# Two attention layers on one core: the result's stores move from GpSimd's queue to SyncE's, and one weight tile moves in SBUF

## The chip, the cores and the metric

The kernel runs on one core of a Trainium2 chip. The metric is the device time of one execution in microseconds; of each kernel several executions are timed and their median is given. A core has five engines that run their own instruction streams: TensorE (PE, matrix products), VectorE (DVE), ScalarE (ACT), GpSimd (POOL) and SyncE (SP). They meet through semaphores. DMAs are issued by an engine's instruction and carried out by 16 DMA engines that all queues share; in this kernel SP and POOL issue all of them.

## The reference

Input is `x`, 48 x 48 positions of 768 channels, in float32. Two layers follow each other, each of the form `x = x + attention(group_norm(x))`, the norm over 32 groups of 24 channels. The attention has 12 heads of 64 channels over all 2304 positions, with two tables of relative positions:

```python
qkv = x @ qkv_w + qkv_b
u = x @ FacTu_w                                   # layer 0 only, rank 16
qkv[..., :C] += u @ q_facts_w @ FacTv_w
qkv[..., 2*C:] += u @ v_facts_w @ FacTv_w
attn = einsum('bqc,bkc->bqk', q * scale, k)
attn += rel_h[:, :, :, :, None] + rel_w[:, :, :, None, :]   # from q and the tables
out = softmax(attn) @ v
return out @ proj_w + proj_b
```

Layer 0 adds low-rank terms to the q and v weights (a 768 x 16 matrix, a 16 x 16 one, a 16 x 768 one). Layer 1 has none; there the weights come transposed.

## The kernel before

`two_layers` (line 56) calls `compute` (line 72) once for the fast form "f". That form takes exponentials without subtracting the maximum first; it stores the reciprocals of the denominators and at the end judges from them whether they all lie in a safe range: `judge` (line 1081) writes one number, `bad`. Every engine loads `bad` (line 63) and branches on it (line 67). Only when it isn't zero does a second form "g" run, with the maxima subtracted. In the runs here it is skipped: each engine jumps over its instructions. Behind the jump, the other side of the branch sets the semaphores to what the skipped form would have left them at: each engine waits for its own semaphore (SP for those of its DMAs, POOL for those of its own) and raises them. Then the program ends: SP waits for all of them (line 1337), and all engines meet in two barriers.

A layer has these stages. In layer 0, `load_transposed` brings `x` in and turns it so that channels lie on the 128 partitions. `group_norm` normalises; `project` computes k and v; `project_q` (line 601) computes q and, from q and the tables, the position terms for rows (`psr`, stored by `rel_h`) and for columns (`psc`, stored by `rel_w`, lines 663 to 684, at the very end of each half of the heads). All of k, v, q and the position terms go to DRAM through POOL's queue. `attend_plain` (line 861) then runs over 6 pairs of heads and, for each pair, 5 blocks of up to 512 queries. A block needs key rows in two float parts (`k`), the queries in two parts (`q`) and three `rel` tiles of position terms, one for each group of 768 keys (`NG` = 3, index g). `fetched` (line 951) issues these loads on SP in the order g = 0, 1, 2; for the first block the keys come in the same three steps. `Block.scores` (line 971) uses `rel[b // 2]`, so that the third `rel` tile serves the last 6 of the 18 key tiles of a block. `out_project` (line 1120) multiplies with `proj_w`, adds the residual, and in layer 1 turns the result back and stores it.

The two sets of buffers of the attention, `in0` and `in1`, reuse memory that earlier stages have left. Pools with `reuse_waits` wait tile by tile: a load into a tile waits for the last readers and writers of the tiles that lay at the same bytes before, and of no others. So where a tile lies decides whom a later load waits for. SP executes its instructions in order, and each of its DMAs signals on one of 8 semaphores in turn; a DMA waits until the one eight places before it has landed.

`Weights` (line 255) holds the small tiles of a layer in a pool of one buffer for each tag, `p0_one`; memory is given out in the order in which tags are first asked for. `begin` (line 276) asks for fu, facts and fv of the low-rank terms, then bt (biases) and for both tables flat and tab, which the position products read until the end of `project_q`. `low_rank` (line 312) multiplies the low-rank factors into `low`, 128 x 2 x 768 numbers, 6144 bytes of each partition; `fold` (line 363) uses `low` to add the low-rank terms to the v and q weights; its last use is in the middle of the first half of `project_q`. `begin` is called again for layer 1, after layer 0's attention.

In the built program the tiles of layer 0 in `p0_one`, and the first attention block's `rel` tiles, lie at these bytes of each partition:

| tile | before |
|---|---|
| fv | 217728 to 220800 |
| bt, flat0, tab0 | 220800 to 222040 |
| flat1, tab1 | 222048 to 223192 |
| low | 223200 to 229344 |
| rel, second group | 214976 to 221120 |
| rel, third group | 221120 to 227264 |
| bt, flat, tab of layer 1 | 226944 to 229336 |

In the last layer `out_project` takes the blocks of 384 positions in three rounds of two. In a round, PE forms seven products for each of three channel tiles; then for each of the 2 x 3 groups of 128 positions PE turns the six channel tiles into `psn`, ACT copies them to a tile `o` of 128 x 768 (six buffers), and POOL issues the store to `out`:

```python
o = op.tile([P, C], F32, tag="o", name=f"o_{b}_{i}_{j}")
nc.scalar.copy(o, ps[:, 0:C])
nc.gpsimd.dma_start(out[ts(pair[i] * TPB + j, P), :], o)
```

All loads of the three rounds stand on SP ahead of this in the built program; the stores are POOL's last DMAs.

Of the kernel before, what the change touches and what calls it, by code (L numbers as in the profile page):

```python
# [9 lines left out]
F32 = mybir.dt.float32  # L10
# [8 lines left out]
P = 128  # L19
C = 768  # L20
# [8 lines left out]
TPB = QB // P  # L29
# [42 lines left out]
def compute(ctx: ExitStack, tc: tile.TileContext, x, layers, out, run, bad):  # L72


    nc = tc.nc
# [22 lines left out]
    for sign, base in ((1, 0), (-1, GSZ - 1)):  # L98
        nc.gpsimd.affine_select(
            out=gin, in_=gin, compare_op=ALU.is_ge, fill=0.0, base=base,  # L100
# [3 lines left out]
            out=gout, in_=gout, compare_op=ALU.is_ge, fill=0.0, base=base,  # L104
# [25 lines left out]
    with ExitStack() as hots:  # L130
# [4 lines left out]
        for i, (rows, pattern, shape) in enumerate(parts):  # L135
# [3 lines left out]
                out=t, in_=t, compare_op=ALU.not_equal, fill=1.0, base=0,  # L139
# [18 lines left out]
    def in_order(instruction):  # L158

        tc.keep_in_program_order(instruction)  # L160
# [94 lines left out]
    class Weights:  # L255
# [20 lines left out]
        def begin(self):  # L276
            one, ly = self.one, self.ly
            if ly.lora is not None:
                u_w, q_f, v_f, o_w = ly.lora
                self.fu = one.tile([P, CT, RANK], F32, tag="fu", name="fu")  # L280
                nc.gpsimd.dma_start(self.fu, u_w.rearrange("(t p) r -> p t r", p=P))
                self.facts = one.tile([RANK, 2, P], F32, tag="facts", name="facts")
                nc.gpsimd.memset(self.facts, 0.0)
                self.out = one.tile([P, C], F32, tag="fv", name="fv")
                for i, f in enumerate((q_f, v_f)):
                    nc.gpsimd.dma_start(self.facts[:, i, 0:RANK], f)
                for r in range(4):
                    nc.gpsimd.dma_start(self.out[r * 32 : r * 32 + RANK, :], o_w)
            self.bt = one.tile([P, 3 * CT], F32, tag="bt", name="bt")
            nc.sync.dma_start(self.bt, ly.qkv_bt)  # L290
            nc.sync.dma_start(v_bias[self.li], ly.qkv_bt[:, 2 * CT :])

            self.tables = []
            for a, src in enumerate((ly.relh_t, ly.relw_t)):
                flat = one.tile([P, REL], F32, tag=f"flat{a}", name=f"flat{a}")
                tab = one.tile([P, REL, 2], F32, tag=f"tab{a}", name=f"tab{a}")
                nc.gpsimd.memset(tab, 0.0)
                for par in range(2):  # L300
                    nc.sync.dma_start(flat[ts(par, HD), :], src)
                self.tables.append((flat, tab))
# [9 lines left out]
        def low_rank(self, room):  # L312


            if self.ly.lora is None:
                return
            fuT = room.tile([RANK, C], F32, tag="x", name="fuT")
            self.low = self.one.tile([P, 2, C], F32, tag="low", name="low")
            for r in range(1, 4):
                nc.gpsimd.tensor_copy(  # L320
                    self.facts[:, :, r * 32 : r * 32 + RANK], self.facts[:, :, 0:RANK]
                )
            for half in range(2):
                cols = ts(half, HP * P)
                ps = self.ps.tile([P, HP * P], F32, tag="f", name=f"psu_{half}")
                for t in range(HP):
                    in_order(nc.tensor.transpose(
                        ps[0:RANK, ts(t, P)], self.fu[:, half * HP + t, :], ident
                    ))
                nc.vector.tensor_copy(fuT[:, cols], ps[0:RANK])  # L330
            for half in range(2):
                yield
                cols = ts(half, HP * P)
                for i in range(2):
                    ps = self.ps.tile([P, HP * P], F32, tag="f", name=f"psl_{half}_{i}")
                    in_order(nc.tensor.matmul(
                        ps, lhsT=self.facts[:, i, :], rhs=fuT[:, cols], start=True, stop=True
                    ))
                    nc.scalar.copy(self.low[:, i, cols], ps)
# [521 lines left out]
    def attend_plain(li, qd, kd, vd, rel_d, od, beside):  # L861
# [11 lines left out]
        with ExitStack() as es:  # L873
# [166 lines left out]
                            self.rec[r * HD : r * HD + 1, :],  # L1040
                        )


            wanted = [fetch_keys(0), fetch_values(0), fetch_queries(0, *blocks[0])]
            keys, queries, v = fetched(wanted[0], wanted[2], wanted[1])
            behind = []
# [73 lines left out]
    def out_project(ly, li, od, w, bt, first, res, xT, next_res, beside):  # L1120


        last = xT is None
        with ExitStack() as es:
            tp = es.enter_context(tc.tile_pool(name="p3_t", bufs=1, **REUSE))
            kp = es.enter_context(tc.tile_pool(name="p3_k", bufs=2, **REUSE))
            rp = es.enter_context(tc.tile_pool(name="p3_r", bufs=2, **REUSE))
            yp = es.enter_context(tc.tile_pool(name="p3_y", bufs=2, **REUSE))
            ps_y = es.enter_context(tc.tile_pool(
                name="ps_y", bufs=4 if last else 8, space=PSUM, **REUSE  # L1130
            ))
            ps_n = None
            if last:
                op = es.enter_context(tc.tile_pool(name="p3_o", bufs=2 * TPB, **REUSE))
                ps_n = es.enter_context(tc.tile_pool(name="ps_n", bufs=2, space=PSUM, **REUSE))
            for at, b in enumerate((1, 0, 2)):
                pair = (b, b + HB)
                if last and not shifted and at == HB - 1:
                    judge(ps_n)
                if not last:  # L1140
                    y = [xT[i] for i in pair]
                elif at == 0:
                    y = first[2:]
                else:
                    y = yp.tile([P, 2, CT, QB], F32, tag="y", name=f"y_{b}")
                    y = [y[:, i] for i in range(2)]
                if at == 0:
                    oT = first[:2]
                else:
                    oT = rp.tile([P, 2, CT, QB], F32, tag="oT", name=f"oT_{b}")  # L1150
                    oT = [oT[:, i] for i in range(2)]
                for i in range(2):
                    fetch_output(oT[i], od, pair[i])

                for i in range(2):
                    nc.sync.dma_start(y[i], res[pair[i]])
                if at == 0:
                    next(beside, None)
                blocks = {
                    f"{i + 1}{j + 1}": oT[j][:, i * HP : (i + 1) * HP]  # L1160
                    for i in range(2) for j in range(2)
                }
                t = tp.tile([P, 4, HP, QB], F32, tag="t", name=f"oT_t_{b}")
                right = sums_of_b(blocks, t)
                for co in range(HP):
                    def product(i):
                        left_of, right_of = FACTORS[i]
                        ps = ps_y.tile([P, QB], F32, tag="y", name=f"psy_{b}_{co}_{i}")
                        for t in range(HP):
                            nc.tensor.matmul(  # L1170
                                ps, lhsT=w[left_of][:, t, ts(co, P)], rhs=right[right_of][:, t, :],
                                start=(t == 0), stop=(t == HP - 1),
                            )
                        return ps

                    def result(at, x, more):
                        i, j = int(at[0]) - 1, int(at[1]) - 1
                        ch = i * HP + co
                        to = y[j][:, ch, :]
                        nc.vector.tensor_add(to, to, more)  # L1180
                        nc.vector.scalar_tensor_tensor(
                            to, x, bt[:, ch : ch + 1], to, ALU.add, ALU.add
                        )
                        if not last:
                            nc.vector.bn_stats(stats[:, ch, pair[j], :], to)

                    seven_products(kp, QB, product, result)
                for _ in beside:
                    pass
                for i in range(2):  # L1190
                    if not last:
                        nc.gpsimd.dma_start(next_res[pair[i]], y[i])
                        continue
                    for j in range(TPB):
                        ps = ps_n.tile([P, 1024], F32, tag="n", name=f"psn_{b}_{i}_{j}")
                        for t in range(CT):
                            nc.tensor.transpose(ps[:, ts(t, P)], y[i][:, t, ts(j, P)], ident)
                        o = op.tile([P, C], F32, tag="o", name=f"o_{b}_{i}_{j}")
                        nc.scalar.copy(o, ps[:, 0:C])
                        nc.gpsimd.dma_start(out[ts(pair[i] * TPB + j, P), :], o)  # L1200

    residuals = [[scratch(f"res{li}_{b}", [P, CT, QB]) for b in range(NQB)] for li in range(2)]
    def begin(li, es):
# [137 lines left out]
```

## Time and profile before

| | us |
|---|---|
| median of 3 runs | 3338.63 (3338.19 to 3340.41) |
| the profiled execution, its own time | 3338.02 |
| its span, first to last instruction | 3336.3 |
| PE busy | 3258.2 (98%) |
| POOL busy | 382.8 (11%) |
| first store of the result issued on POOL, last | 3223.2, 3316.7 |
| last instruction of SP that loads data | 3196.3, for 1.7 |
| PE's wait for `rel` in the first block of layer 0 | 4.8 |

The profile shows one execution. Its own time is 1.7 us over the span of its instructions. Busy time of PE is taken from the records of its products; issuing a DMA isn't counted as busy on SP, and a semaphore wait isn't counted on any engine. In lists of groups, "A <- B" names what an instruction writes and reads, "SPq" or "POOLq" an instruction of that engine's sequencer. A DMA has two times: how long its issue held the engine, and when it landed. "L1200" is line 1200 of the kernel before.

### The profile page before, as it was taken

To read this page: it belongs to the slowest core of one execution; us is meant where nothing else is said; L and a number is where in the kernel's file an instruction comes from. 1 tells how busy PE (TensorE), PEld (TensorE's weight loads), DVE (VectorE), ACT (ScalarE), POOL (GpSimd) and SP (SyncE) were. 2 spreads that over 40 slices of the span, in tenths; PEclk is the share of its full clock that TensorE was granted. 3 is DMA by queue.
4 is the path that set the end of the run, shared out by engine and by line. 5 is a ranking of instruction groups with operands and counts; after the bars stand their busy time and mean duration, and the time that the engine had idled before them with its cause. 6 is when DMAs were issued, how large, how long until landed. Compare 5 with 4: busy or idle time off the path is not lost.

```text
span 3336.3 us, 50056 instructions
## 1 busy us (share of the span) xinstructions
PE 3258.2 (98%) x19708; PEld 2002.1 (60%) x19708; DVE 2103.0 (63%) x2275; ACT 1422.4 (43%) x1655; POOL 382.8 (11%) x719
## 2 busy tenths in 40 slices
PE   8999999999999999999989999999999999999997
PEld 5556665565656565656555566656565656565654
DVE  8432446777777677777774234677777767767653
ACT  3101345555555555553011024655555555555511
POOL 2144110000000000000012531100000000000000
PEclk9999999999999999999999999999999999999998
DMA  7333479453436353425234346863534444533241
GB/s 261 128 85 84 135 226 250 85 111 93 121 74 141 73 125 90 106 64 172 86 135 137 56 120 201 244 158 89 123 82 125 90 119 94 121 83 86 86 145 58
DMA packets 221202, 405.60 MB, mean 122 GB/s; under 512 B 41584, under 2 KB 109072, under 8 KB 217120
## 3 DMA queue, kind: packets, MB, share of 16 engines
q1 hardware_dynamic: 178656, 253.00, 31.1%
q0 software_dynamic: 42304, 149.31, 14.0%
q8 instruction: 159, 2.61, 0.3%
q14 instruction: 83, 0.68, 0.1%
HBM read 253.27 MB, written 148.89 MB: 121 GB/s over the span
## 4 chain that ended last, share of the span: by engine, by line
PE 85%; issue 7%; ACT 2%; DVE 2%; DMA 2%; POOL 1%; SPq 1%; POOLq 0%; ACTq 0%; DVEq 0%
PE ps_sc L960 33%; PE ps_ov L960 25%; PE ps_q L695 8%; PE ps_v L521 7%; PE ps_k L521 4%; PE psy L1170 4%; ACT pt L987 1%; PE psr L635 1%; PE ps_d L960 1%; DMA rel<-f_r 1%; PE psc L635 1%; POOL f_k L565 1%; DVE relw L390 0%; ACT relw L389 0%; POOL out_dram L1200 0%
## 5 line engine op out<-in xcount | busy, mean ns | idle before, releaser
L993 DVE TENSOR_TENSOR sum<-sum,pt 128x1024 f32<-128x1024 f32 (+1 forms) x960 | 1072.6, 1117 | 317.2 <-ACT pt L987 233.6
L987 ACT ACTIVATE pt<-ps_sc 128x1024 f32<-128x1024 f32 (+1 forms) x1080 | 990.6, 939 | 660.6 <-PE ps_sc L960 600.4
L960 PE MATMUL ps_sc<-q,k 64*128 64x512 f32 (+1 forms) x8640 | 1096.3, 373 | 9.6 <-ACT pt L987 8.1
L960 PEld LDWEIGHTS ps_sc<-q,k 64*128 64x128 f32 x8640 | 774.2, 185 | 273.8 <-issue 92.0
L960 PE MATMUL ps_ov<-pt,v 128*64 128x512 f32 (+1 forms) x4320 | 883.9, 554 | 0.0
L960 PEld LDWEIGHTS ps_ov<-pt,v 128*64 128x64 f32 x4320 | 293.5, 137 | 475.2 <-issue 436.1
L960 PE MATMUL ps_sc<-rel,places 64*128 64x512 f32 (+1 forms) x2160 | 412.3, 371 | 4.8 <-DMA rel<-f_r 4.8
L695 PE MATMUL ps_q<-xT,w_q 128*128 128x384 f32 x864 | 285.5, 489 | 0.6 <-DVE v L585 0.6
L1038 POOL DMA_DIRECT2D f_rec<-rec x120 | 58.3, 490 | 1951.2 <-DVE rec L1027 1950.9
L1027 DVE RECIPROCAL rec<-ps_d 128x512 f32<-128x512 f32 (+1 forms) x60 | 182.2, 3036 | 100.0 <-PE ps_d L960 100.0
L960 PEld LDWEIGHTS ps_sc<-rel,places 64*128 64x128 f32 x2160 | 211.2, 185 | 34.4 <-DMA rel<-f_r 5.1
L695 PEld LDWEIGHTS ps_q<-xT,w_q 128*128 128x128 f32 x864 | 163.2, 191 | 110.4 <-issue 2.9
L599 POOL DMA_DIRECT2D f_v<-v x288 | 137.3, 485 | 105.8 <-DVE v L585 94.2
L701 DVE TENSOR_SCALAR x_q<-ps_q,bt 128x384 f32<-128x384 f32 x72 | 44.4, 617 | 163.3 <-PE ps_q L695 163.3
L521 PE MATMUL ps_k<-xt,w_k 128*128 128x384 f32 x432 | 143.4, 487 | 3.6 <-DVE xt L425 2.6
L521 PE MATMUL ps_k<-xT,w_k 128*128 128x384 f32 x324 | 116.2, 512 | 4.7 <-DVE xT L248 4.6
L521 PEld LDWEIGHTS ps_k<-xt,w_k 128*128 128x128 f32 x432 | 81.5, 190 | 63.0 <-PE ps_k L521 3.0
L1002 ACT CAST sum<-sum 128x1024 bf16<-128x1024 f32 (+1 forms) x60 | 57.6, 960 | 132.3 <-DVE sum L993 132.3
L1005 DVE TENSOR_TENSOR sum<-sum,sum 128x1024 bf16<-128x1024 f32 (+1 forms) x60 | 67.1, 1119 | 61.6 <-ACT sum L1004 61.6
L1003 DVE TENSOR_TENSOR sum<-sum,sum 128x1024 f32<-128x1024 f32 (+1 forms) x60 | 67.1, 1119 | 61.6 <-ACT sum L1002 61.6
L993 DVE TENSOR_TENSOR sum<-pt 128x1024 f32<-128x1024 f32 (+1 forms) x60 | 67.1, 1118 | 47.3 <-ACT pt L987 46.2
L384 ACT ACTIVATE xs_q<-x_q 128x1152 fp32r<-128x1152 f32 x24 | 27.9, 1164 | 161.5 <-DVE x_q L701 153.6
(186 smaller groups left out, 2416.9 us busy)
## 6 DMA issues: line engine op xcount, KB each, us to landing
rel<-f_r SPq DMA_DIRECT2D x1152, 96.0 KB, 4.1
f_k<-xs POOLq DMA_DIRECT2D x72, 384.0 KB, 2.9
f_q<-xs_q POOLq DMA_DIRECT2D x48, 576.0 KB, 3.8
k<-f_k SPq DMA_DIRECT2D x72, 384.0 KB, 5.8
q<-f_q SPq DMA_DIRECT2D x96, 256.0 KB, 3.0
f_r<-relh POOLq DMA_DIRECT2D x48, 432.0 KB, 5.0
f_r<-relw POOLq DMA_DIRECT2D x8, 2592.0 KB, 18.2
f_v<-v POOLq DMA_DIRECT2D x288, 48.0 KB, 2.0
```

The costliest lines, as they stand in the source:

```text
L521: nc.tensor.matmul(ps, lhsT=x, rhs=y, start=(t == 0), stop=(t == HP - 1))
L599: nc.gpsimd.dma_start(vd[to : to + KG, :], v[ts(r, KG), k])
L635: nc.tensor.matmul(ps[:, i, :, :], lhsT=weights.tables[a][:, 2 * s : 2 * (s + HG)], rhs=lines_of(l0 + i), start=True, stop=True,)
L695: nc.tensor.matmul(ps, lhsT=w[:, t, ts(pr, P)], rhs=xT[b][:, t, :], start=(t == 0), stop=(t == CT - 1),)
L960: in_order(nc.tensor.matmul(*args, **kwargs))
L987: nc.scalar.activation(pt, ps[:, :, 0 : self.n], AF.Exp)
L993: nc.vector.tensor_add(self.sum, self.first if kt == 1 else self.sum, pt)
L1003: nc.vector.tensor_sub(self.sum, self.sum, hi)
L1005: nc.vector.tensor_sub(lo, self.sum, mid)
L1027: nc.vector.reciprocal(self.rec, ps)
L1038: nc.gpsimd.dma_start(recs[li][2 * self.pair + r : 2 * self.pair + r + 1, to], self.rec[r * HD : r * HD + 1, :],)
L1170: nc.tensor.matmul(ps, lhsT=w[left_of][:, t, ts(co, P)], rhs=right[right_of][:, t, :], start=(t == 0), stop=(t == HP - 1),)
```

## The change

Two things are changed. The 18 stores of the result are issued by SP in place of POOL. And the tile `low` is asked for in `Weights.begin`, ahead of bt and the tables, in place of `low_rank`, so that it lies at bytes 220800 to 226944 and bt, flat and tab of layer 0 lie behind it, at 226944 to 229336, where those of layer 1 lie too. What is computed, and the order of the instructions on PE, DVE and ACT, stays; so does the size of the pool. In the new file, lines 285 to 317 stand one lower down, and those behind line 1042 one higher up.

```diff
@@ -282,6 +282,7 @@
                 self.facts = one.tile([RANK, 2, P], F32, tag="facts", name="facts")
                 nc.gpsimd.memset(self.facts, 0.0)
                 self.out = one.tile([P, C], F32, tag="fv", name="fv")
+                self.low = one.tile([P, 2, C], F32, tag="low", name="low")
                 for i, f in enumerate((q_f, v_f)):
                     nc.gpsimd.dma_start(self.facts[:, i, 0:RANK], f)
                 for r in range(4):
@@ -315,7 +316,6 @@
             if self.ly.lora is None:
                 return
             fuT = room.tile([RANK, C], F32, tag="x", name="fuT")
-            self.low = self.one.tile([P, 2, C], F32, tag="low", name="low")
             for r in range(1, 4):
                 nc.gpsimd.tensor_copy(
                     self.facts[:, :, r * 32 : r * 32 + RANK], self.facts[:, :, 0:RANK]
@@ -1197,7 +1196,7 @@
                             nc.tensor.transpose(ps[:, ts(t, P)], y[i][:, t, ts(j, P)], ident)
                         o = op.tile([P, C], F32, tag="o", name=f"o_{b}_{i}_{j}")
                         nc.scalar.copy(o, ps[:, 0:C])
-                        nc.gpsimd.dma_start(out[ts(pair[i] * TPB + j, P), :], o)
+                        nc.sync.dma_start(out[ts(pair[i] * TPB + j, P), :], o)
```

## The prediction

> **What bounds the kernel now.** I read the page first, then the chain of waits by stretches, then the two places that the change touches: the end of the program and the start of layer 0's attention. Line 1 of the page says that PE bounds nearly everything; a change to DMAs counts only where PE waits for one, or after PE's last product.
>
> ```profile
> span 3336.3 us, 50056 instructions
> PE 3258.2 (98%) x19708; PEld 2002.1 (60%) x19708; DVE 2103.0 (63%) x2275; ACT 1422.4 (43%) x1655; POOL 382.8 (11%) x719
> ```
>
> PE is idle for 3336.3 - 3258.2 = 78 us. The timeline's last rows put 20 us of that at the end: after ACT's copy at 3315.56 + 0.80 = 3316.36 nothing but stores and sequencer work is left. The stores' own view, and the views of lines 67 and 1337 (the end of the branch on `bad`, the end of the program; a "q" marks a sequencer's instruction, the numbers are ns min/median/max, then first and last start):
>
> ```profile
> L1200 POOL DMA_DIRECT2D out_dram<-o x18: 539/539/549, 3223.2 to 3316.7; - x18
> DMA to landing us min/median/max: 2.6/3.8/5.6
> ...
> L67 SPq EVENT_SEMAPHORE  x8: 17/17/17, 3277.5 to 3278.0; - x8
> L67 POOLq EVENT_SEMAPHORE  x5: 17/43/43, 3321.8 to 3322.4; - x5
> L67 SPq COMPARE_BRANCH  x1: 45/45/45, 3273.3 to 3273.3; - x1
> L67 POOLq COMPARE_BRANCH  x1: 54/54/54, 3317.8 to 3317.8; - x1
> L67 POOLq INC_SWDGE_SEM  x1: 2682/2682/2682, 3322.5 to 3322.5; - x1
> ...
> L1337 SPq EVENT_SEMAPHORE  x14: 17/28/28, 3325.1 to 3336.2; - x14
> L1337 POOLq DRAIN  x3: 46/107/10277, 3325.2 to 3336.0; - x3
> ```
>
> The reader is to see the tail as a row: the last store is issued at 3316.65 and lands 5.6 us later, at 3322.25; only then do POOL's five waits end (3322.4); then come INC_SWDGE_SEM, 2.68 us, and a DRAIN of 10.28 us (3325.16 to 3335.44); the last barriers take 3336.3 - 3335.5 = 0.8 us. Some 13 us stand on POOL alone, after everything has landed. SP passed its own eight waits of line 67 already at 3278.
>
> At the other place (SP's timeline, its waits from 495 to 530 us, PE's timeline):
>
> ```profile
> 501.04 1.73 SPq L897 DMA_DIRECT2D k<-f_k  x2
> 504.33 0.32 SPq L941 DMA_DIRECT2D rel<-f_r  x1
> 506.59 1.11 SPq L945 DMA_DIRECT2D rel<-f_r  x1
> 508.57 1.61 SPq L941 DMA_DIRECT2D rel<-f_r  x1
> 510.22 2.06 SPq L945 DMA_DIRECT2D rel<-f_r  x1
> ...
> SPq L941 <- PE psc L635: 1.5, 1, 1.5
> ...
> 529.94 0.76 PE L960 MATMUL ps_sc<-rel,places 64*128 64x512 f32 x1 [4.83 <-DMA rel<-f_r]
> ```
>
> SP waits 1.5 us for the last position product before it loads the third group of the first block's rel rows; PE later waits 4.83 us for the last of these eight loads.
>
> **What the Trainium skill says.** "DMA: Bandwidth & Descriptors", section "Latency and other measured facts", gives a first byte after about 0.6 us for SP's path and 1 us for POOL's. In this trace's DMA packets the first data starts 0.95 us after an undisturbed issue on SP (q at 470.24) and 1.12 us after POOL's at 3312.42: same order, a smaller gap. Its section "Queues, rings and completion order" has each DMA engine take turns between queues by packets; the trace agrees: while POOL's 27648-byte packets of `f_r<-relw` move (about 1.1 us each), SP's queue falls from 155 packets per us (at 507 us) to between 6 and 20 (510 to 521). "Runtime: NRT & Kernel Launch", "Instruction fetch mechanics": a taken branch out of the fetched pages waits for a fetch. Here the next instruction stands 4.0 us after POOL's branch and 4.1 after SP's. "VectorE: DVE Perf Modes", "The DRAIN you can't avoid", knows boilerplate DRAINs of about 12 ns on all engines; that holds for SP, ACT, DVE and PE here (7 to 17 ns), not for POOL's 10277 ns, and the trace decides.
>
> **The change part by part.** The order of work on PE, DVE and ACT is untouched; 18 stores leave POOL's program and stand behind SP's last load.
>
> *Stores, the way there.* SP issues its last load at 3196.3 and the first store is due at 3223, so no load stands behind a store. Each needs one issue on SP (0.3 to 0.45 us, rows of the k and rel loads) against ACT's two copies per 1.77 us: it keeps pace. ACT's copies wait for buffers of an earlier round, which landed some 40 us before. The first two rounds lie beside PE's products: 0.
>
> *Stores, the last round.* POOL's first issue came 0.29 us after its copy (3312.13 to 3312.42); SP's releases take 0.02 us, and the first data comes 0.17 us sooner: data starts about 0.45 us earlier. The six stores are 2.36 MB. The three rounds took 8.66, 8.75 and 9.83 us from first issue to last landing on POOL; six key loads of the same shape on SP took 8.9 (2692.49) to 9.7 us (2345.94). I take 9.3: 3312.15 + 9.3 = 3321.4, against 3322.25. No store on SP is in this trace; bounds 8.5 and 14 us (POOL's 3072-byte packets of `f_v<-v` took 268 ns in the mean; six stores are 48 such packets per DMA engine, 12.9 us).
>
> *SP's own way out* is now behind the last store: issue 3316.4 to 3316.85, load of `bad` 0.79 (its time before), branch 0.05, fetch 4.1 (bounds 3.1, DVE's, and 5.5, PE's branch row): 3321.8. Landing and fetch end together. Eight waits, 0.53 us (3277.49 to 3278.02): 3322.3. Twelve waits of line 1337, 0.71 us before (3325.08 to 3325.79), hidden then behind POOL's DRAIN and exposed now: 3323.1. Two drains and the gather, 0.1; last barriers 0.8: 3324.0.
>
> *POOL's way out.* Its last DMA is the block's output at 3182.28, landed at 3184.8. It loads `bad` when that is written (3272.48, SP's time before), branches, fetches, passes its waits at about 3278, and needs 2.68 + 10.28 us: done near 3291, 30 us ahead of the end, beside PE's last round. What these 13 us are for the trace doesn't show; if their length hangs on the stores, they only get shorter. The stores' removal therefore gives 3336.3 - 3324.0 = 12.3 us.
>
> *The `low` tile.* In the built program `low` (6144 bytes per partition) moves from byte 223200 to 220800, and bt, flat and tab of layer 0 go up by the same 6144. Of the first attention block's buffers the second rel group (214976 to 221120) and the third (221120 to 227264) lie over them. Before, the third lay on both tables, hence the wait for the last position product; after, it lies on `low`, bt and the start of flat0, and waits for the last use of bt, the q bias at 484.4, long past. So its first load can go when the key loads are out (501.60 + 1.16 = 502.76) and the DMA eight places earlier on SP has landed (502.07): 502.8 for 504.33, 1.5 us earlier. Loads 2 to 6 are held by the landings of the second group (502.43, 502.78, 503.66, 505.28, 506.39) and gain 1.5 down to 0.2. Loads 7 and 8 wait for the landings of the two key loads, 508.55 and 509.68, both ahead of them in the same queue: they stay. PE waits for load 8. Between 505 and 508 the DMA engines are full with SP's queue anyway; what is issued earlier lines up behind the keys. I take 0 for it. Bounds: -4.8 (the stall goes; next late would be block 1's first rel group, landed at 536.8, just before PE would come for it) and +1. The other waits changed by the move are for work of layer 0 long done when layer 1's tables are laid out: 0.
>
> *Sum*: span 3324.0. The profiled execution took 3338.02, 1.7 over its span: 3325.7. It was 0.6 under the median of the three runs (3338.63); against that, 3338.63 - 12.3 = 3326.3.
>
> **The rivals.**
> A, as summed: 3326.3, own range 3324.5 to 3329 (fetch and landing).
> B, as A, and the stall at 525 us goes as well: 3321.5. For it: layer 1, whose tables always lay at the upper bytes, shows no such stall (first score to first denominator 44.2 us, 2130.5 to 2174.7, against 50.1 in layer 0). Against: there all loads of the third group were out by 2126.9, before the relw store.
> C, SP's stores move in slow 3072-byte packets: data ends at 3313.1 + 12.9 = 3326.0, landing 3326.4, end 1.8 later, 3328.2: 8.1 gained, 3330.5. Against: the key loads' 3072-byte packets took 136 ns.
> D, the DRAIN is not POOL's stores' but follows the last DMA wherever it was issued, on SP now: 3324.0 + 10.3 = 3334.3, 3336.6: no change. For it: no DRAIN shortly after a DMA on SP is in the trace (its 7 to 13 ns came 120 us after). Against: the DRAIN begins when every landing has been seen.
> E, slower: the earlier rel loads push the key loads of the third group behind the relw store, which starts to move at 508.0. Place: SP's queue, 502 to 510 us; price: about 1.2 us for each packet of SP that a DMA engine still owes by then. The two key loads are 16 packets per engine, 19 us when all of them slip: -12.3 + 19 = +7, 3345.6. It decides the sign from about 10 packets on, slower by 0.2% only with all 16. Against: the keys are issued first, in the same queue.
>
> **How the numbers follow.** A 0.69, B 0.09, C 0.10, D 0.09, E 0.03. Time 3326.3. The range takes B's end and C's: 3321 to 3331; left out are D, E and the outer ends. What a measurement of this kernel tells from no change is about 0.2%, 6.7 us: faster A + B + C = 0.88, same D = 0.09, slower E = 0.03.
>
> **What would show it.** Right: POOL's long DRAIN between 3278 and 3292; SP's waits of line 67 ending near 3322, and the span about 1.7 us behind them; the `psc` wait of SP gone, load 8 of the third group still landing near 529.8 and PE's 4.8 us in place. Wrong: a DRAIN of 10 us on SP or behind the last landing (D), a last landing after 3324 (C), PE's wait at 525 gone (B) or over 10 us (E).

## The result and the profile after

| | before | after |
|---|---|---|
| median, us | 3338.19 (3336.60 to 3340.41) | 3324.31 (3321.71 to 3326.59) |
| profiled execution, its span, us | 3338.02, 3336.3 | 3326.59, 3324.8 |
| end of ACT's last copy to the end of the span, us | 3316.36 to 3336.29: 19.93 | 3318.09 to 3324.80: 6.71 |
| first issue to last landing, last round, us | 9.83 | 9.17 |

The ratio is 0.996 with a 95% interval of 0.9945 to 0.9974; the medians differ by 13.9 us. The page of the kernel after begins:

```profile
span 3324.8 us, 50057 instructions
PE 3260.4 (98%) x19708; PEld 1999.5 (60%) x19708; DVE 2103.2 (63%) x2275; ACT 1423.2 (43%) x1655; POOL 373.1 (11%) x701
```

PE's busy time is no shorter (3260.4 against 3258.2): what went is idle time, and nearly all of it stood in the tail, behind PE's last product. It shows in three views of the kernel after. First the stores:

```profile
L1199 SPq DMA_DIRECT2D out_dram<-o x18: 332/332/1352, 3224.7 to 3318.1; - x18
DMA to landing us min/median/max: 2.3/3.6/5.0
```

Then line 67, where the branch on `bad` ends:

```profile
L67 SPq EVENT_SEMAPHORE  x8: 17/17/17, 3322.6 to 3323.1; - x8
L67 POOLq EVENT_SEMAPHORE  x5: 17/42/43, 3278.0 to 3278.3; - x5
...
L67 POOLq COMPARE_BRANCH  x1: 54/54/54, 3275.2 to 3275.2; - x1
L67 POOLq INC_SWDGE_SEM  x1: 2322/2322/2322, 3278.4 to 3278.4; - x1
L67 SPq COMPARE_BRANCH  x1: 45/45/45, 3319.6 to 3319.6; - x1
```

And the end of the program, line 1336:

```profile
L1336 SPq EVENT_SEMAPHORE  x14: 17/28/28, 3323.2 to 3324.7; - x14
...
L1336 POOLq DRAIN  x3: 46/107/8807, 3280.8 to 3324.5; - x3
L1336 SPq DRAIN  x3: 7/7/13, 3323.9 to 3324.2; - x3
```

The engines have changed places. POOL takes its branch at 3275.2, and its semaphore instruction and long DRAIN run from 3278.4 to 3280.8 + 8.8 = 3289.6, beside PE's last round. SP is now the late one: branch at 3319.6, last landing at 3323.05, twenty waits to 3323.9, and DRAINs of 7 to 13 ns, although its last DMA had landed only 0.9 us earlier. From ACT's last copy to the end that is 19.93 - 6.71 = 13.2 us less.

The profiled spans differ by less, 11.5 us, because ACT's last copy ends 1.73 us later after than before. The whole of that stands already at the start of layer 0's attention, where the time from the first score to the first denominator is 52.3 us after and 50.1 before; the experiments below tell whether the move of `low` did it.

### The profile page after: what moved, and what is told of

Same layout as the page of the kernel before. It is cut to its first block, busy times and chain, and to the rows that moved or that the text cites. A ratio compares the mean times of both kernels' runs of the same rounds, so it can differ in the third digit from the quotient of the medians.

```text
span 3324.8 us, 50057 instructions
## 1 busy us (share of the span) xinstructions
PE 3260.4 (98%) x19708; PEld 1999.5 (60%) x19708; DVE 2103.2 (63%) x2275; ACT 1423.2 (43%) x1655; POOL 373.1 (11%) x701
## 3 DMA queue, kind: packets, MB, share of 16 engines
q0 software_dynamic: 40864, 142.23, 13.5%
## 4 chain that ended last, share of the span: by engine, by line
PE 89%; issue 3%; DVE 2%; ACT 2%; DMA 2%; POOL 1%; SPq 1%; ACTq 0%; POOLq 0%; DVEq 0%
PE ps_sc L960 33%; PE ps_ov L960 25%; PE ps_q L695 8%; PE ps_v L521 7%; PE psy L1169 7%; PE ps_k L521 4%; ACT pt L987 1%; PE psr L635 1%; PE ps_d L960 1%; DMA rel<-f_r 1%; PE psc L635 1%; POOL f_k L565 1%; DVE relw L390 0%; ACT relw L389 0%; PE psn L1196 0%
## 5 line engine op out<-in xcount | busy, mean ns | idle before, releaser
L521 PEld LDWEIGHTS ps_k<-xT,w_k 128*128 128x128 f32 x324 | 64.7, 203 | 54.9 <-DVE xT L248 9.4
```

Source lines behind the costliest of these rows:

```text
L521: nc.tensor.matmul(ps, lhsT=x, rhs=y, start=(t == 0), stop=(t == HP - 1))
```

## Experiments

### Each part of the change alone

Only the stores on SP:

```
-                        nc.gpsimd.dma_start(out[ts(pair[i] * TPB + j, P), :], o)
+                        nc.sync.dma_start(out[ts(pair[i] * TPB + j, P), :], o)
```

> The 18 stores of the result on SyncE, the low-rank tile asked for where it was. Theory (all of the gain is POOL's way out, the tile's move is worth nothing): about 3325 us, 12 to 14 us under the kernel before, the same as the full change within its scatter of 2 us; in layer 0 SyncE waits again for the last position product and PE's wait for the third group's last rel load is near 4.8 us. Rival 1 (the tile's move costs 1 to 2 us, as layer 0's first block of the profiled full change suggests): about 3322.5. Rival 2 (the tile's move carries part of the gain): 3327 or more.

Only the tile:

```
+                self.low = one.tile([P, 2, C], F32, tag="low", name="low")
...
-            self.low = self.one.tile([P, 2, C], F32, tag="low", name="low")
```

> The low-rank tile ahead of the tables alone, the stores on GpSimd as before. Theory: 3338, the kernel before within 1 us; SyncE's wait for the position product gone, PE's wait for rel loads in layer 0's first block 4 to 5 us as before. Rival 1 (it costs): 3339 to 3340. Rival 2 (the stall of 4.8 us goes, B of the prediction): 3333.

The stores alone: 3326.37 us (3321.27 to 3326.96), ratio 0.996, interval 0.9947 to 0.9974, 6.71 us from the last copy to the end, as in the full change. The tile alone: 3337.30 us beside 3338.54 before, ratio 0.9997, interval 0.9989 to 1.0005. The gain is the stores'; the tile's move is nothing that can be told from zero, and a stall of 4.8 us did not go.

Nor did the move cost the 2.2 us that layer 0's first block lost in the profiled run of the full change: that block takes 52.6 us with the stores alone, where `low` lies as before, and 52.4 with the tile alone. The 50.1 us of the profile before was the odd value; why is told under the cut stores.

### One store left on POOL

```
-                        nc.sync.dma_start(out[ts(pair[i] * TPB + j, P), :], o)
+                        by = nc.gpsimd if (b, i, j) == (2, 1, TPB - 1) else nc.sync
+                        by.dma_start(out[ts(pair[i] * TPB + j, P), :], o)
```

> The full change, but the very last of the 18 stores stays on GpSimd, 17 are on SyncE. Theory (POOL can leave only behind its last own store, and then pays 2.5 us for its semaphore instruction and 9 to 10 us for its DRAIN, however few its stores are): all of the gain is back, 3336 to 3338, with the long DRAIN ending within 1 us of the span's end. Rival 1 (the DRAIN's length is set by how many stores GpSimd issued or how many are still under way): a DRAIN of 1 to 4 us, 3327 to 3331. Rival 2 (the 13 us belong to the whole program's last landings and were hidden for another reason): 3325.

It took 3336.65 us beside 3338.54, ratio 0.9995, interval 0.9986 to 1.0003: one store of 18 gives the gain back. Line 67 and the end of the program of this run:

```profile
L67 POOLq INC_SWDGE_SEM  x1: 2342/2342/2342, 3320.8 to 3320.8; - x1
```

```profile
L1338 POOLq DRAIN  x3: 46/107/8888, 3323.2 to 3332.7; - x3
```

POOL leaves behind its own last store, and then pays. But both lengths are shorter than before, 8888 ns for 10277 and 2342 for 2682. With 17 DMAs fewer on POOL that is 82 and 20 ns for each; to the full change, one DMA fewer still, it is 81 and 20. The length goes by something that POOL had issued.

### Only the last round on SP

```
-                        nc.gpsimd.dma_start(out[ts(pair[i] * TPB + j, P), :], o)
+                        by = nc.sync if b == 2 else nc.gpsimd
+                        by.dma_start(out[ts(pair[i] * TPB + j, P), :], o)
```

> The full change, but only the last round's six stores on SyncE, the twelve ahead of them on GpSimd (681 DMAs there). Theory: GpSimd's DRAIN 8.81 + 12 x 0.082 = 9.8 us and its semaphore instruction 2.56 us, done by 3293 and hidden beside PE's last round: 3324 to 3326, as the full change. Rival (SyncE must carry all 18 for the gain, or GpSimd is held until the last stores land): 3330 or more.

It took 3325.61 us (ratio 0.9959, interval 0.9943 to 0.9974), with a DRAIN of 9787 ns and a semaphore instruction of 2566 ns, the two lengths that the count had given, and both done by 3291.0. The place of the last round is what matters, not the number of stores. The way out was longer than in the full change, 8.31 us for 6.71: the last of SP's eight waits began at 3323.85, 1.26 us behind the seventh, although all of SP's stores had landed by 3322.32. The trace has a packet of its kind `instruction` from 3322.62 to 3323.67, which may be what SP waited for; no run tests it. The medians, 3325.61 and 3324.31, don't tell the two kernels apart.

### The packets that starve layer 0's loads

The stores of the column positions, cut into nine each. There are eight such stores, in both layers and both halves of the heads, and all are cut; the edit stands on top of the full change:

```
                 for found, part in zip(rel_d[1][half], parts):
-                    nc.gpsimd.dma_start(found, part.bitcast(F32))
+                    for t in range(HP * 3):
+                        piece = (slice(None), t // 3, ts(t % 3, N // 3))
+                        nc.gpsimd.dma_start(found[piece], part.bitcast(F32)[piece])
```

> The full change, and each store of the column positions (rows of 27648 bytes) cut into nine of 3072 bytes a row, so that SyncE's rel loads get their turn on the DMA engines at the start of layer 0's attention. Theory (the big packets starve the loads, and PE's 4 to 5 us there are theirs): the wait of PE for rel loads falls under 1 us and the time is 4 to 5 us less than that of the full change, about 3319.5. Rival 1 (the loads are late by their volume, whatever the packets): the wait stays, 3324. Rival 2 (the stall goes but block 1's loads come late in turn): 3321 to 3323, with a new wait of 1 to 3 us on ps_sc in block 1.

It took 3318.36 us (3317.05 to 3320.24), ratio 0.9941, interval 0.9927 to 0.9954: about 6 us less than the full change, and the two ranges do not touch. The last rel row of the third group lands at 514.49 instead of 530.94. PE's waits between 495 and 560 us (us in total, times, longest), in the full change and then in this run:

```profile
PE ps_sc L960 <- DMA rel<-f_r: 5.1, 2, 4.3
PE psc L635 <- DVE relw L390: 1.7, 3, 1.2
```

```profile
PE psc L635 <- DVE relw L390: 1.8, 3, 1.2
PE ps_sc L962 <- ACT pt L989: 0.6, 1, 0.6
```

The waits on DMA are gone. That POOL's stores merely came later in this run is not the reason. From 510 to 514 us, packets, MB and share of the two queues, in the full change and then here:

```profile
q0 software_dynamic: 57, 1.58, 95.0%
q1 hardware_dynamic: 63, 0.11, 7.4%
```

```profile
q0 software_dynamic: 319, 1.48, 89.6%
q1 hardware_dynamic: 130, 0.20, 13.3%
```

POOL's queue (q0) moved nearly as much here, in rows of 3072 bytes of which the trace shows two to a packet, 6144 bytes; SP's (q1) got twice as many packets through between them.

The block gained more than the waits measured, though: from the first score to the first denominator it takes 43.3 us, not 52.3. These 9.0 us are all that the profiles show: the last copy ends 8.8 us sooner, so the cuts in the other half and in layer 1 gave nothing that can be seen. The table of stretches has the other half: stretch, its length, PE's busy time and matmuls, PE's granted clock, the DMA engines' share and their GB/s. Before, after, and with cut stores:

```profile
525.00:531.00 6.00, 1.17 (x7) 0.89 0.54 166
531.00:537.00 6.00, 6.00 (x46) 0.82 0.60 148
```

```profile
525.00:531.00 6.00, 0.90 (x5) 0.95 0.53 164
531.00:537.00 6.00, 5.97 (x28) 0.50 0.51 130
537.00:545.00 8.00, 8.00 (x49) 0.99 1.09 161
```

```profile
525.00:531.00 6.00, 6.00 (x48) 1.00 0.64 172
531.00:537.00 6.00, 6.00 (x38) 1.00 0.98 151
```

Behind the stall PE runs at half its clock for 6 us in the profile after: its eight products of q and k take 2.46 us there, 1.08 to 1.19 us from 545 us on.

```profile
531.03 0.76 PE L960 MATMUL ps_sc<-rel,places 64*128 64x512 f32 x1 [4.27 <-DMA rel<-f_r]
531.03 2.46 PE L960 MATMUL ps_sc<-q,k 64*128 64x512 f32 x8
...
546.59 1.08 PE L960 MATMUL ps_sc<-q,k 64*128 64x512 f32 x8
```

Asked for narrower stretches, the trace before shows 0.50 from 529.71 to 533.12, 3.41 us, in which PE is busy for 3.18; the trace after shows it from 530.37 to 537.20, 6.83 us, with PE busy for 6.17. Half of the 2.99 us more is 1.5 us, most of the 1.73 us that the last copy came later. In the other profiles with whole stores it stood at 0.50 for 6.8 us, and for 10.24 us in the one with only the stores moved. So the stall costs its own 4 to 5.6 us and then, in these two profiles, 1.6 and 3.1 us of slow clock; how long it is slow changes from one execution to the next. With cut stores the clock is 1.00 throughout, and both costs are gone.

### Cut stores without the tile's move

> The run with the cut stores, but the low-rank tile asked for where it was before, so that SyncE waits 1.5 us for the last position product before the third group of rel rows. Theory (the move of the tile is worth nothing, even when the loads are no longer starved): 3318 to 3319, as with the move, PE's wait for rel loads under 1 us. Rival (with the starving gone this wait is the one that ends last): PE waits 1 to 2 us, 3319.5 to 3320.5.

It took 3318.24 us (3317.04 to 3319.22), ratio 0.9939, interval 0.9924 to 0.9954, with no wait of PE for rel rows and 43.3 us for the first block. SP's wait for the last position product hides even when nothing starves the loads.

### The result's stores on POOL again, the others cut

```
-                        nc.sync.dma_start(out[ts(pair[i] * TPB + j, P), :], o)
+                        nc.gpsimd.dma_start(out[ts(pair[i] * TPB + j, P), :], o)
```

> The run with the cut stores of the column positions, but the result's stores on GpSimd again. GpSimd issues 751 DMAs. Theory of counting: DRAIN 0.8 + 18 x 0.082 = 2.3 us, semaphore instruction 0.37 + 18 x 0.02 = 0.73; against the cut-store run (3318.4) the end is later by these 3.0 us and by POOL's slower last round (about 1 us): 3322.5. Rival (GpSimd's way out is 13 us whenever the last store is its own): 3331 to 3333.

The run with cut stores and the result's stores on SP had these lines of POOL, and this run the third:

```profile
L67 POOLq INC_SWDGE_SEM  x1: 367/367/367, 3269.5 to 3269.5; - x1
L1339 POOLq DRAIN  x3: 46/107/803, 3269.9 to 3316.1; - x3
```

```profile
L1339 POOLq DRAIN  x3: 46/107/2273, 3315.2 to 3318.0; - x3
```

There the DRAIN was 803 ns and the semaphore instruction 367 ns, with 733 DMAs on POOL where the full change has 669. This run has 751, and shows 2273 and 727 ns: 18 x 81.7 and 18 x 20 ns more, as expected. It took 3319.38 us (3317.49 to 3322.21), ratio 0.9944, interval 0.9929 to 0.9959, some 3 us less than the 3322.5 expected. Stores on POOL cost 10.0 us from the last copy to the end here, against 7.05 on SP and 19.93 before: most of the change's gain is had with no store moved to SP.

### What POOL counts

46 small DMAs on POOL added to the kernel before, which makes 733 too:

```
+            if last and not shifted:
+                spare = scratch("spare", [46, HP * GH])
+                for n in range(46):
+                    nc.gpsimd.dma_start(
+                        spare[n : n + 1, :], gin[n : n + 1].rearrange("p a b -> p (a b)")
+                    )
```

> The kernel before (stores on GpSimd), with 46 small DMAs of one row each more on GpSimd between the attention's end and the first store; they write to a buffer of their own and lie in GpSimd's idle time. GpSimd then issues 733 DMAs, as many as the run with the cut stores (687 before, 669 in the full change). Theory (GpSimd's last DRAIN and semaphore instruction grow by 82 and 20 ns for each DMA it has issued and fall back at some count between 687 and 733): DRAIN near 0.8 us, the semaphore instruction near 0.37, so 11.8 us less with the stores still on GpSimd: about 3326.5. Rival 1 (it is descriptors or bytes that count, not DMAs): DRAIN 10.3 to 14.1 us, 3338 to 3343. Rival 2 (the short DRAIN of the cut-store run has to do with the stores being on SyncE): DRAIN 10.3, 3338.

It took 3339.41 us, ratio 1.0001, interval 0.9992 to 1.0009. The 46 DMAs did not stand where I meant them: with nothing to wait for, they were laid at 14.3 to 80.5 us of the span. The DRAIN took 10195 ns and the semaphore instruction 2662 ns, each one DMA's step less than before. So it is not the number of DMAs issued since the start, nor is 733 a number at which the count falls. The first rival comes nearest (it had 10.3 us or more): what the DMAs consist of matters.

The other variant has few DMAs of many elements:

```
+            if last and not shifted:
+                spare = scratch("spare", [P, 5, 2 * CT])
+                for n in range(5):
+                    nc.gpsimd.dma_start(spare[:, n, 0 : 2 * CT : 2], bt)
```

> The kernel before, stores on GpSimd, with five DMAs more on GpSimd during layer 1's attention, each of 128 x 6 single elements of 4 bytes, so 768 elements each; they write to a buffer of their own. Theory 1 (the way out grows with every DMA on GpSimd, here 692 after 687): DRAIN 10.28 + 5 x 0.082 = 10.7 us, semaphore instruction 2.8, 3338 to 3339. Theory 2 (both lengths count the DMAs since GpSimd last filled a ring of descriptors; the runs so far fit a ring that comes round every 1145 elements per DMA engine, at the 550th DMA of the kernel before, and in the cut-store run a fourth time 20 DMAs ahead of its end; other sizes fit nearly as well): the ring comes round once more, 10 to 30 DMAs ahead of the end, DRAIN 0.3 to 2 us, semaphore instruction 0.2 to 0.8, so 10 to 12 us less with the stores still on GpSimd: 3326 to 3329.

It took 3325.28 us (3324.54 to 3327.20), ratio 0.9958, interval 0.9944 to 0.9972: five DMAs of 3 KB each, 1100 us ahead of the end, are worth as much as the whole change. The DMAs themselves, line 67 and the end of the program of this run:

```profile
L1139 POOL DMA_DIRECT2D f_spare<-bproj x5: 828/828/866, 2221.0 to 2224.3; - x5
```

```profile
L67 POOLq COMPARE_BRANCH  x1: 54/54/54, 3317.6 to 3317.6; - x1
L67 POOLq INC_SWDGE_SEM  x1: 587/587/587, 3322.3 to 3322.3; - x1
```

```profile
L1341 POOLq DRAIN  x3: 46/107/1702, 3322.9 to 3325.2; - x3
```

The stores are still POOL's, POOL still branches at 3317.6 and still leaves last, but its two instructions take 2.3 us in place of 13.0. Theory 1 falls: it had 10.7 us for the DRAIN. The idea of a ring gave the right order (0.3 to 2 us), and the Trainium skill ("DMA: Bandwidth & Descriptors", section "SWDGE vs HWDGE vs iDMA") says that GpSimd appends the descriptors of its DMAs to rings; but no run shows the ring itself, and the size that I had fitted is wrong: it put this run 11 DMAs below the cut-store run, and (1702 - 803) / 81.7 puts it 11 above. Shown is that the count begins anew somewhere, and that neither the number of DMAs decides where (46 more moved it by one) nor the bytes (the cut stores move the same bytes as the whole ones). The number of elements fits all runs in kind; after how many of them it begins anew stays open. Of the 13.5 us of this run's median the tail explains 19.93 - 9.31 = 10.6. The two profiled spans differ by 10.8, so the tail is all that these two executions show; the rest of the median is not accounted for.

### A second queue in the last round

On top of the cut stores, without the tile's move:

```
+                        by = nc.scalar if b == 2 and (i * TPB + j) % 2 else nc.sync
+                        by.dma_start(out[ts(pair[i] * TPB + j, P), :], o)
```

> The cut-store run without the tile's move, and in the last round every second store issued by ScalarE instead of SyncE. Theory (the last landing is set by the bytes that the DMA engines have still to move, and SyncE's fetch behind its branch ends with it): nothing gained, 3317.5 to 3319.5, ScalarE's copies at most 0.3 us later. Rival (one queue is what limits the last round): the last landing 1 to 2 us sooner after the first issue than the 9.0 us of one queue, 3316.5 to 3317.

It took 3318.10 us (3316.97 to 3322.57), ratio 0.9936, interval 0.9921 to 0.9952: no difference from one queue that these runs can tell. The last landing comes 8.76 us after the first issue, against 8.97 and 8.66 us in the two runs with cut stores and one queue. The way out is 6.49 us against 7.05, half a microsecond. A queue is not what limits the last round. Nor would a sooner landing have shortened this run: the last store landed at 3318.71, and SP, still fetching behind its branch, began the eight waits at 3318.52 and came to the last of them at 3319.05.

## Why the prediction was right, and where it was not

*The tail's place.* Right. What stood behind the last landing was POOL's, followed POOL's last store and no other DMA, and was hidden once POOL had no store in the last round: done at 3289.6, where the prediction had "near 3291". One store left on POOL and the last round alone on SP show it from both sides. D fell with SP's DRAINs of 7 to 13 ns, directly behind a landing.

*The stores on SP.* Right. 9.17 us from first issue to last landing for the 9.3 taken; C's 12.9 us of slow packets did not come: on SP the stores' 3072-byte packets took 128 ns in the mean, for the 268 that C had.

*SP's way out.* The mechanism was right, the size of one term was not: the fetch behind SP's branch was taken as 4.1 us, from SP's own row before, with a lower bound of 3.1. It took 2.97 (3319.60 to 3322.56). The load of `bad` took 0.98 for 0.79. Landing and fetch were to end together; the fetch ended last in effect. The eight waits behind it took the 0.53 us that they had taken before (3322.56 to 3323.09), and the last landing, at 3323.05, came just ahead of the wait for it. From the last copy to the end the prediction had 3324.0 - 3316.4 = 7.6 us; it is 6.71.

*POOL's 13 us.* "If their length hangs on the stores, they only get shorter" held here (12.96 to 11.13 us) and is wrong as a rule. Each DMA less takes off 102 ns only until the count begins elsewhere, and five DMAs more took off 10.7 us (12.96 to 2.29). The prediction treated the 13 us as a price of having stores on POOL; they were the price of having them there with a long count.

*The `low` tile.* Right that it is worth nothing, and for the reason given: the first load goes at 502.65 (502.8 taken), the two held loads still go last, the eighth lands at 530.94, PE's waits stay at 5.1 us. B fell. E fell too: the key loads landed at 509.08 and 510.47, for 508.55 and 509.68 before.

*The sum.* 3326.3 was forecast, 3324.31 measured. In the profiled execution the span came out 0.8 us over the 3324.0 of the sum, from two misses that cancel: 0.9 us less in the tail, 1.7 more ahead of it. That the span came within 1 us of the sum is luck to that extent. The second was not in the sum at all: the clock behind the stall, at which the prediction did not look. With it, B was priced too low. The stall was taken as 4.8 us; without it the block is 9 us shorter in the profiles, and the medians are 6 us lower with the tile moved and 8 without (3318.24 for 3326.37).

## What to carry to other kernels

Look at what each engine still has to do behind its own last landing. If one of them pays at its exit, as POOL does here, let it have its last DMA early: here one store left behind was enough to lose the whole gain. A long wait of PE is to be priced with the clock of the stretch behind it, not by its own length. Where two queues meet, look at the size of the packets on each: here it decided how late the other queue's loads were, and cutting the stores was worth 6 to 8 us where letting the loads go sooner was worth nothing.

## What was not expected of the hardware

- GpSimd's semaphore instruction and DRAIN at the end of the program grow by 20 and 82 ns with each DMA, and begin anew somewhere: 2682 and 10277 ns before, 367 and 803 in the run with cut stores, 587 and 1702 with five DMAs of 768 single elements added to the kernel before.
- Behind the stall of 4 to 5.6 us the clock stands at 0.50 for 3.4 to 10.2 us (3.41 before, 6.83 after, 10.24 with the stores alone). The Trainium skill ("TensorE: Matmul & The Clock Gate", section "HAM oscillation — how this bites in real kernels") has the rule "no PE-idle gaps >~3.4µs", with the clock halved behind a longer one; the traces agree here. They also show it behind less: in the profile before PE waits 2.42 us until 3174.40 and 1.07 us until 3175.78, and the clock stands at 0.50 from 3175.05 to 3181.85.
- Packets of 27648 bytes on POOL's queue held SP's last rel row until 530.94 us; cut to rows of 3072 bytes (packets of 6144), with the same bytes to move, it landed at 514.49.
